# Attention block: weight products by seven instead of eight block products (Strassen), with block sums on VectorE and GpSimd

## The chip, the cores and the metric

The kernel runs on one core of one Trainium2 chip. The metric is the device time of one execution in microseconds (us); a kernel's time is the median of its runs. In the profile PE is TensorE's matmuls, PEld its weight loads, DVE is VectorE, ACT is ScalarE, POOL is GpSimd and SP is SyncE, which issues most DMAs.

## The reference

There are 16 images of 512 channels and 32 x 32 pixels, all in fp32. Each is normalised in 8 groups of channels, goes through a 1x1 convolution to q, k and v, through attention with 4 heads of 128 channels over the 1024 pixels, and through a 1x1 projection that is added to the input.

```python
xg = x.reshape(b, NUM_GROUPS, -1)
xn = ((xg - mu) * jax.lax.rsqrt(var + EPS)).reshape(b, c, h, w)
xn = xn * norm_gamma[:, None, None] + norm_beta[:, None, None]
qkv = jnp.einsum('oc,bchw->bohw', qkv_w, xn) + qkv_b[:, None, None]
...
attn = jax.nn.softmax(jnp.einsum('bhnd,bhmd->bhnm', q, k) * scale, axis=-1)
out = jnp.einsum('bhnm,bhmd->bhnd', attn, v)
...
out = jnp.einsum('oc,bchw->bohw', proj_w, out) + proj_b[:, None, None]
return x + out
```

## The kernel before

An image is held as four tiles x of 128 channels x 1024 pixels. The work is a chain of steps s, one for each image b, head h and block j of 128 keys (16 x 4 x 8 = 512 steps). A step computes the scores of a block for all 1024 queries (`scores`, L280: two matmuls of 128x512), their exponential on ScalarE (L285, tile p), the running sum of p on VectorE (L291, tile tot), and one step later the weighted sum of v (`weighted_sum`, L321: two matmuls into tile po). After the eighth block of a head `denominators` turns tot into row sums: a transpose of 32x32 blocks and a reduction on VectorE (L298, L300), a small matmul l against `fold` on PE (L302), a reciprocal r, and two DMAs that spread the reciprocals over all partitions (tile rinv). `divide` (L330) multiplies the head's output o with it.

Between the scores and the weighted sums stand the products with the weights, put there by `plan_head`, which gives each block j of a head a list of units. A unit is one PSUM bank of 512 columns with four matmuls, one for each 128 input channels: `qk_unit` (L231, tile pqk, read by ScalarE at L235), `v_unit` (L243, tile pv, read by VectorE at L248), `proj_unit` (L252, tile pp, read at L259 together with bias and residual). q and k of head h + 1 are made during head h; v and the first q and k of the next image during the last head of this one; the projection of an image during the first head of the next. All these units, the small matmul l, and the two matmuls of the normalisation's group means (pm and pv at L48 and L59, 4 columns each) share the two banks of the pool `ps_a`.

The next image's statistics come during head 2 (`stats_chunk`, `stats_group`), its normalisation at the start of head 3 (`normalise`: VectorE subtracts and scales at L71, ScalarE adds beta at L75), into tiles xn of its own, so that x stays for the residual. At the end, six projection units of the last image run with three of four matmuls before the last `divide`.

The order in which engines work is that of the program as the tile scheduler has arranged it; each engine runs its instructions in order and waits on semaphores.

```python
for s in range(steps + 1):
    if s < steps:
        ...
        scores(s)
        for u in plan[j]:
            u()
        if j == 1 and s > NB:
            divide(*where(s - NB)[:2])
    if s > 0:
        if s % NB == 0:
            denominators(*where(s - 1)[:2])
        weighted_sum(s - 1)
```

The last branch of the program (`general_path`) runs only when a flag, worked out from the row sums, asks for it.

## Time and profile before

| | |
|---|---|
| median of 3 runs | 3590.45 us (3590.2 to 3592.93) |
| the profiled execution | 3592.27 us, of which the trace spans 3590.2 us |
| PE busy | 3555.8 us, 99% of the span |
| VectorE, ScalarE, GpSimd busy | 1150.2, 824.6, 16.6 us |
| granted TensorE clock | 0.999 of full speed |
| DMA | 106.80 MB |

The span is what the trace covers; the execution's own time is 2.1 us longer. A busy share is an average over the whole span and says nothing of where an engine waits. An fp32 matmul leaves two records in the trace, one for each pass over its columns, each with a weight load of its own.

### The profile page before, as it was taken

How to read it: one execution, taken by the hardware profiler on the slowest of the kernel's cores; microseconds unless marked ns; L12 is line 12 of the kernel's file. 1: busy time of each engine (PE TensorE's matmuls, PEld its weight loads, DVE VectorE, ACT ScalarE, POOL GpSimd, SP SyncE). 2: the span in 40 equal slices, each digit the busy share in tenths (PEclk: the TensorE clock that was granted, in tenths of full speed). 3: DMA queues.
4: the chain of work that ended last, by engine and by line, in shares of the span. 5: the costliest groups of instructions: out<-in, count | busy, mean ns of one | idle time of the engine just before them, and what ended most of it. 6: DMA issues, size and time to landing. Idle time of an engine off the chain costs nothing.

```text
span 3590.2 us, 20812 instructions
## 1 busy us (share of the span) xinstructions
PE 3555.8 (99%) x8386; PEld 1567.8 (44%) x8386; DVE 1150.2 (32%) x1471; ACT 824.6 (23%) x893; POOL 16.6 (0%) x22
## 2 busy tenths in 40 slices
PE   8999999999999999999999999999999999999999
PEld 3444444444444444444444444444444444444443
DVE  2333323333232332423324233332333323233223
ACT  1221212212132121312213122131221312213121
POOL 0000000000000000000000000000000000000000
PEclk9999999999999999999999999999999999999999
DMA  2001001010000100001010010100101001010001
GB/s 73 36 12 53 12 27 38 12 53 12 30 35 12 53 12 30 36 15 50 12 38 29 16 47 12 53 18 12 53 6 59 12 15 50 6 59 12 18 24 36
DMA packets 43062, 106.80 MB, mean 30 GB/s; under 512 B 8016, under 2 KB 8016, under 8 KB 42960
## 3 DMA queue, kind: packets, MB, share of 16 engines
...
q8 instruction: 67, 1.10, 0.1%
q14 instruction: 35, 0.29, 0.0%
HBM read 71.58 MB, written 33.82 MB: 29 GB/s over the span
## 4 chain that ended last, share of the span: by engine, by line
PE 95%; DVE 2%; ACT 1%; DMA 0%; POOL 0%; issue 0%; SPq 0%; POOLq 0%
PE pqk L231 25%; PE po L321 23%; PE s L280 23%; PE pv L243 12%; PE pp L252 12%; ACT xn L75 1%; PE pp_last L252 1%; DVE tt L298 1%; DVE tot L291 1%; DVE part L300 1%; POOL rstd L63 0%; ACT p L285 0%; PE l L302 0%; DVE xn L71 0%; DMA wq<-in_qkv_wT 0%
## 5 line engine op out<-in xcount | busy, mean ns | idle before, releaser
L321 PE MATMUL po<-p,v 128*128 128x512 f32 x2048 | 972.0, 596 | 0.0
L291 DVE TENSOR_TENSOR tot<-tot,p 128x1024 f32<-128x1024 f32 x384 | 470.6, 1225 | 1565.1 <-ACT p L285 1564.9
L280 PE MATMUL s<-qk,qk 128*128 128x512 f32 x2048 | 966.4, 593 | 0.0
L285 ACT ACTIVATE p<-s 128x1024 f32<-128x1024 f32 x512 | 523.2, 1022 | 1760.5 <-PE s L280 1659.3
L280 PEld LDWEIGHTS s<-qk,qk 128*128 128x128 f32 x2048 | 387.8, 190 | 482.8 <-issue 482.2
L321 PEld LDWEIGHTS po<-p,v 128*128 128x128 f32 x2048 | 382.9, 190 | 455.0 <-issue 437.2
L231 PE MATMUL pqk<-xn,wq 128*128 128x512 f32 x1024 | 460.2, 595 | 3.8 <-DMA wproj<-in_proj_wT 3.8
L231 PE MATMUL pqk<-xn,wk 128*128 128x512 f32 x1024 | 457.7, 592 | 0.0
L243 PE MATMUL pv<-wv,xn 128*128 128x512 f32 x1024 | 449.4, 592 | 0.0
L252 PE MATMUL pp<-o,wproj 128*128 128x512 f32 x976 | 430.6, 594 | 1.5 <-DVE y L259 1.5
L235 ACT ACTIVATE qk<-pqk,qkb_sb 128x512 f32<-128x512 f32 x256 | 175.9, 687 | 838.1 <-PE pqk L231 838.1
L231 PEld LDWEIGHTS pqk<-xn,wq 128*128 128x128 f32 x1024 | 195.4, 191 | 249.7 <-issue 245.3
L231 PEld LDWEIGHTS pqk<-xn,wk 128*128 128x128 f32 x1024 | 194.6, 190 | 244.9 <-issue 244.9
L243 PEld LDWEIGHTS pv<-wv,xn 128*128 128x128 f32 x1024 | 194.6, 190 | 244.9 <-issue 244.9
L252 PEld LDWEIGHTS pp<-o,wproj 128*128 128x128 f32 x976 | 186.0, 191 | 236.3 <-issue 233.9
L259 DVE SCALAR_TENSOR_TENSOR y<-pp,projb_sb,x 128x512 f32<-128x512 f32 x122 | 91.6, 751 | 236.7 <-PE pp L252 236.7
L248 DVE TENSOR_TENSOR v<-pv,vb_sb 128x512 f32<-128x512 f32 x128 | 88.3, 690 | 231.8 <-PE pv L243 231.8
L289 DVE TENSOR_TENSOR tot<-p,p 128x1024 f32<-128x1024 f32 x64 | 78.4, 1225 | 178.6 <-ACT p L285 178.6
L39 DVE BATCH_NORM_STATS2 st<-x 128x6 f32<-128x512 f32 x128 | 80.8, 663 | 5.2 <-DMA x<-in_x 5.1
L330 DVE TENSOR_TENSOR o<-o,rinv 128x1024 f32<-128x1024 f32 x64 | 78.1, 1220 | 9.9 <-DMA rinv<-row 9.8
L327 ACT COPY o<-po 128x1024 f32<-128x1024 f32 x64 | 64.6, 1009 | 69.1 <-PE po L321 69.1
L298 DVE STREAM_TRANSPOSE tt<-tot 128x1024 f32<-128x1024 f32 x64 | 79.7, 1245 | 2.2
...
## 6 DMA issues: line engine op xcount, KB each, us to landing
...
out_y<-y SPq DMA_DIRECT2D x128, 256.0 KB, 2.0
...
```

The source lines that it names most:

```text
L39: nc.vector.bn_stats(st[:, h, :], x[:, ts(h, HALF)])
L231: nc.tensor.matmul(acc, wqkv[which][c][:, ts(h, P)], xns[b, c][:, ts(half, HALF)], start=(c == 0), stop=(c == NCC - 1),)
L235: nc.scalar.activation(store[b, h][:, ts(half, HALF)], acc, AF.Identity, bias=qkb_sb[:, o : o + 1])
L243: nc.tensor.matmul(acc[:, :C], xns[b, c][:, ts(j, P)], wqkv[2][c], start=(c == 0), stop=(c == NCC - 1),)
L248: nc.vector.tensor_add(vs[b, j], acc[:, :C], vb_sb)
L252: nc.tensor.matmul(acc, wproj[c][:, ts(o, P)], os_[b, c][:, ts(half, HALF)], start=(c == 0), stop=(c == NCC - 1),)
L259: nc.vector.scalar_tensor_tensor(y, acc, projb_sb[:, o : o + 1], xs[b, o][:, ts(half, HALF)], ALU.add, ALU.add)
L280: nc.tensor.matmul(sc[:, ts(half, HALF)], ks[b, h][:, ts(j, P)], qs[b, h][:, ts(half, HALF)], start=True, stop=True,)
L285: e = nc.scalar.activation(ps[s], sc, AF.Exp, scale=SCALE)
L291: nc.vector.tensor_add(tot[b, h], tot[b, h], ps[s])
L298: nc.vector.transpose(tt.rearrange("p c m -> p (c m)"), t)
L321: nc.tensor.matmul(po[b, h][:, ts(half, HALF)], vs[b, j][:, ts(h, P)], p[:, ts(half, HALF)], start=(j == 0), stop=(j == NB - 1),)
```

## The change

Each product with the weights is seen as a product of 2 x 2 blocks and done with seven block products in place of eight. Of the weights the blocks are a11 to a22, of the data b11 to b22 (two tiles of channels, half of the pixels); s1 to s4 and t1 to t4 are sums of them, made on VectorE for the data (`sums_of_b`, 8 adds of 128x512 for an image's x and 8 for the head outputs o), and once at the start on VectorE and GpSimd for the weights. `quad` is a group of seven products p1 to p7, each of two 128x512 matmuls (for v four of 128x256); they use the two banks of `ps_a`, and what a bank holds is read and added to others by VectorE (u2, u3 and the four results) or, for p1 and one result, ScalarE. p2, p4 and p3 add onto a bank whose first content has been read.

t1 overwrites a half of x or o; x itself is normalised in place, so `proj_units` loads x again from HBM for the residual, and GpSimd adds three of its four results. The pool of x has four tiles in place of eight, and load_x(b + 1) stands in head 2. The bias of v is multiplied with the projection at the start (16 matmuls of one column, L547) and added to that of the projection. The row sums' small matmul becomes three adds of 32x32 and a transpose on VectorE. `divide` moves to block 2. The projection at the end is done whole, after the last divide.

```diff
+FACTORS = {
+    1: ("a11", "b11"), 2: ("a12", "b21"), 3: ("s4", "b22"), 4: ("a22", "t4"),
+    5: ("s1", "t1"), 6: ("s2", "t2"), 7: ("s3", "t3"),
+}
+KC = 2
...
+def sums_of_b(eng, b):
+    for k in range(KC):
+        eng.tensor_sub(b["t3"][k], b["b22"][k], b["b12"][k])
+        eng.tensor_sub(b["t1"][k], b["b12"][k], b["b11"][k])
+        eng.tensor_sub(b["t2"][k], b["b22"][k], b["t1"][k])
+        eng.tensor_sub(b["t4"][k], b["b21"][k], b["t2"][k])
...
-    xpool = ctx.enter_context(tc.tile_pool(name="x", bufs=2 * NCC))
-    xnpool = ctx.enter_context(tc.tile_pool(name="xn", bufs=NCC))
...
+    xpool = ctx.enter_context(tc.tile_pool(name="x", bufs=NCC))
+    tpool = ctx.enter_context(tc.tile_pool(name="t", bufs=1))
...
-    ppool = ctx.enter_context(tc.tile_pool(name="p", bufs=4))
+    ppool = ctx.enter_context(tc.tile_pool(name="p", bufs=3))
...
-    def normalise(b, c):
-        xns[b, c] = xnpool.tile([P, N], F32, tag="xn", name=f"xn_{b}_{c}")
-        norm.apply(xns[b, c], xs[b, c], *scaled[b], c, b > 0)
+    def normalise(b, c, half=None):
+        t = xs[b, c] if half is None else xs[b, c][:, ts(half, HALF)]
+        norm.apply(t, t, *scaled[b], c, True)
...
+    def quad(name, mm, results, shape=None):
+        banks = {}
+        def bank(i):
+            banks[i] = ps_a.tile([P, HALF], F32, tag="acc", name=f"{name}_{i}")
+            return banks[i]
+        def p1():
+            mm(bank(1), 1, True)
+            u["p1"] = upool.tile([P, HALF], F32, tag="p1", name=f"{name}_p1")
+            nc.scalar.copy(u["p1"], banks[1])
+        def p6():
+            mm(bank(6), 6, True)
+            u[2] = upool.tile([P, HALF], F32, tag="u2", bufs=2, name=f"{name}_u2")
+            nc.vector.tensor_add(u[2], banks[6], u["p1"])
+        def p2():
+            mm(banks[1], 2, False)
+            results["c11"](banks[1])
+        def p7():
+            mm(bank(7), 7, True)
+            u[3] = upool.tile([P, HALF], F32, tag="u3", name=f"{name}_u3")
+            nc.vector.tensor_add(u[3], banks[7], u[2])
+        def p5():
+            mm(bank(5), 5, True)
+            results["c22"](banks[5], u[3])
+        def p4():
+            mm(banks[7], 4, False)
+            results["c21"](banks[7], u[2])
+        def p3():
+            mm(banks[5], 3, False)
+            results["c12"](banks[5], u[2])
+        u = {}
+        return [p1, p6, p2, p7, p5, p4, p3]
...
+    def v_units(b, jj):
+        def mm(acc, i, first):
+            wn, xn = FACTORS[i]
+            for g in range(2):
+                for k in range(KC):
+                    nc.tensor.matmul(
+                        acc[:, ts(g, HC)], xb[b][xn][k][:, ts(2 * jj + g, P)], wv[wn][k],
+                        start=(first and g == 0 and k == 0), stop=(k == KC - 1),
+                        skip_group_check=True,
...
+        def plus(which, half):
+            def f(acc, u):
+                t = upool.tile([P, HALF], F32, tag="yu", bufs=2, name=f"yu_{b}_{o}_{which}_{half}")
+                nc.vector.scalar_tensor_tensor(t, acc, bias(which), u, ALU.add, ALU.add)
+                nc.gpsimd.tensor_add(res[which, half], res[which, half], t)
+                store(which, half)
+            return f
...
-        l = ps_a.tile([P, HALF], F32, tag="acc", name=f"l_{b}_{h}")
-        nc.tensor.matmul(l[:BLK, :BLK], part, fold, start=True, stop=True)
-        r = lpool.tile([BLK, BLK], F32, tag="r", name=f"r_{b}_{h}")
-        nc.vector.reciprocal(r, l[:BLK, :BLK])
-        worst = lpool.tile([BLK, BLK], F32, tag="worst", name=f"worst_{b}_{h}")
-        i = b * HEADS + h
-        nc.vector.scalar_tensor_tensor(
-            worst, l[:BLK, :BLK], 1.0, r, ALU.mult, ALU.max, accum_out=spans[:, i : i + 1]
-        )
+        l = lpool.tile([BLK, 4, BLK], F32, tag="l", name=f"l_{b}_{h}")
+        nc.vector.tensor_add(l[:, 0, :], part[ts(0, BLK), :], part[ts(1, BLK), :])
+        nc.vector.tensor_add(l[:, 1, :], part[ts(2, BLK), :], part[ts(3, BLK), :])
+        nc.vector.tensor_add(l[:, 2, :], l[:, 0, :], l[:, 1, :])
+        nc.vector.transpose(l[:, 3, :], l[:, 2, :])
+        r = lpool.tile([BLK, BLK], F32, tag="r", bufs=2, name=f"r_{b}_{h}")
+        nc.vector.reciprocal(r, l[:, 3, :])
...
         if h == 0:
+            spread(plan, qk_units(b, 1), 0, NB)
             if b > 0:
-                spread(plan, proj_units(b - 1), 3, 7)
+                plan[3].append(lambda: o_sums(b - 1))
+                spread(plan, proj_units(b - 1, 0), 4, NB)
+        elif h == 1:
+            if b > 0:
+                spread(plan, proj_units(b - 1, 1), 0, 4)
+            spread(plan, qk_units(b, 2), 0, NB)
+        elif h == 2:
+            spread(plan, qk_units(b, 3), 0, 4)
             if b + 1 < B:
-                plan[7].append(lambda: load_x(b + 1))
-        if h + 1 < HEADS:
-            spread(plan, qk_units(b, h + 1), 0, NB)
-        if b + 1 < B:
-            if h == HEADS - 2:
-                spread(plan, [lambda c=c: stats_chunk(b + 1, c) for c in range(NCC)], 2, 6)
-                plan[6].append(lambda: stats_group(b + 1))
-            if h == HEADS - 1:
-                spread(plan, [lambda c=c: normalise(b + 1, c) for c in range(NCC)], 0, 2)
-                spread(
-                    plan,
-                    qk_units(b + 1, 0) + [lambda j=j: v_unit(b + 1, j) for j in range(NB)],
-                    2, NB,
-                )
+                plan[4].append(lambda: load_x(b + 1))
+                spread(plan, [lambda c=c: stats_chunk(b + 1, c) for c in range(NCC)], 5, 8)
+                plan[7].append(lambda: stats_group(b + 1))
+        elif b + 1 < B:
+            spread(plan, [lambda c=c: normalise(b + 1, c) for c in range(NCC)], 0, 1)
+            plan[0].append(lambda: x_sums(b + 1))
+            spread(
+                plan, qk_units(b + 1, 0) + v_units(b + 1, 0) + v_units(b + 1, 1), 1, NB
+            )
         return plan
...
+    sums_of_a(nc.vector, wqk, ts(0, P))
+    sums_of_a(nc.gpsimd, wv, slice(0, HC))
+    sums_of_a(nc.gpsimd, wqk, slice(P, C))
...
-    for acc, (o, half) in zip(accs, early):
-        proj_products(acc, B - 1, o, half, range(NCC - 1))
-    divide(B - 1, HEADS - 1)
-    for acc, (o, half) in zip(accs, early):
-        proj_products(acc, B - 1, o, half, [NCC - 1])
-        proj_store(acc, B - 1, o, half)
...
+    divide(B - 1, HEADS - 1)
+    o_sums(B - 1)
+    for u in proj_units(B - 1, 0) + proj_units(B - 1, 1):
+        u()
```

The first place is PE at the start of a last head, of image 5, where image 6 is brought in. Before (s and po are scores and weighted sums, l_2 the row sums of head 2, pqk_0_0_0 the first product of the new image's q):

```order
L280 MATMUL s_3690<-qk_5_3_3550,qk_5_3_3623 128x512 x2
L321 MATMUL po_2_3583<-p_3685,v_7_3253 128x512 x2
L280 MATMUL s_3719<-qk_5_3_3550,qk_5_3_3623 128x512
L302 MATMUL l_2_3705<-fold,part_2_3703 32x32
L280 MATMUL s_3719<-qk_5_3_3550,qk_5_3_3623 128x512
L321 MATMUL po_3_3733<-p_3693,v_0_3180 128x512 x2
L280 MATMUL s_3736<-qk_5_3_3550,qk_5_3_3623 128x512 x2
L231 MATMUL pqk_0_0_0_3743<-xn_0_3695,wq_66 128x512
L231 MATMUL pqk_0_0_0_3743<-xn_1_3698,wq_67 128x512
L231 MATMUL pqk_0_0_0_3743<-xn_2_3726,wq_68 128x512
L231 MATMUL pqk_0_0_0_3743<-xn_3_3729,wq_69 128x512
```

After (qk_0_1 and qk_0_6 are the banks of p1 and p6 of the group; what reads x_2 and x_3 into qk_0_1 is p2, and xt are sums of x):

```order
L445 MATMUL s_4398<-qk_5_3_4283,qk_5_3_4303 128x512 x2
L489 MATMUL po_2_4290<-p_4369,v_1_3822 128x512 x2
L445 MATMUL s_4446<-qk_5_3_4283,qk_5_3_4303 128x512 x2
L319 MATMUL qk_0_1_4453<-x_0_4327,wqk_a_0_128 128x512
L319 MATMUL qk_0_1_4453<-x_1_4329,wqk_a_1_129 128x512
L445 MATMUL s_4470<-qk_5_3_4283,qk_5_3_4303 128x512 x2
L319 MATMUL qk_0_6_4458<-xt_4411,wqk_s_0_138 128x512
L319 MATMUL qk_0_1_4453<-x_2_4331,wqk_a_0_130 128x512
L319 MATMUL qk_0_6_4458<-xt_4412,wqk_s_1_139 128x512
L319 MATMUL qk_0_1_4453<-x_3_4333,wqk_a_1_131 128x512
L489 MATMUL po_3_4467<-p_4401,v_1_3822 128x512 x2
L319 MATMUL qk_0_7_4477<-xt_4413,wqk_a_0_132 128x512
```

The row sums' matmul is gone, p1 stands one step earlier, and p6, which needs the sums xt, is split by halves with p2.

The second place is VectorE there. Before (sc is the last small tile of the normalisation, L71 subtracts and scales):

```order
L65 TENSOR_TENSOR sc<-rstd,gamma_sb 128x4
L71 TENSOR_SCALAR xn_0_3695<-x_0_3427,mu,sc 128x1024
L71 TENSOR_SCALAR xn_1_3698<-x_1_3429,mu,sc 128x1024
L71 TENSOR_SCALAR xn_2_3726<-x_2_3431,mu,sc 128x1024
L71 TENSOR_SCALAR xn_3_3729<-x_3_3433,mu,sc 128x1024
L291 TENSOR_TENSOR tot_2_3580<-tot_2_3580,p_3685 128x1024
L298 STREAM_TRANSPOSE tt_2_3701<-tot_2_3580 128x1024
L300 TENSOR_REDUCE part_2_3703<-tt_2_3701 128x32
```

After, behind the transpose L462 and the first three of the same four L71:

```order
L71 TENSOR_SCALAR x_3_4333<-x_3_4333,mu,sc 128x1024
L464 TENSOR_REDUCE part_2_4427<-tt_2_4425 128x32
L467 TENSOR_TENSOR l_2_4429<-part_2_4427 32x32
L468 TENSOR_TENSOR l_2_4429<-part_2_4427 32x32
L156 TENSOR_TENSOR xt_4413<-x_2_4331,x_0_4327 128x512
L469 TENSOR_TENSOR l_2_4429<-l_2_4429 32x32
L157 TENSOR_TENSOR x_0_4327<-x_0_4327 128x512
L156 TENSOR_TENSOR xt_4414<-x_3_4333,x_1_4329 128x512
L158 TENSOR_TENSOR xt_4411<-x_2_4331,x_0_4327 128x512
L157 TENSOR_TENSOR x_1_4329<-x_1_4329 128x512
L159 TENSOR_TENSOR xt_4415<-x_2_4331,xt_4411 128x512
L158 TENSOR_TENSOR xt_4412<-x_3_4333,x_1_4329 128x512
```

Between the last L71 and the sums xt_4411 and xt_4412 that p6 reads (both L158) now stand the reduction of the row sums, their small adds and the other sums of x.

The third place is PE at the end. Before (pp_last are the projection units of the last image; those of o_3, the last head, come after what is shown):

```order
L280 MATMUL s_9809<-qk_15_3_9632,qk_15_3_9696 128x512 x2
L321 MATMUL po_3_9766<-p_9804,v_6_9336 128x512 x2
L321 MATMUL po_3_9766<-p_9812,v_7_9343 128x512 x2
L252 MATMUL pp_last_9835<-o_0_9547,wproj_78 128x512
L252 MATMUL pp_last_9835<-o_1_9655,wproj_79 128x512
L302 MATMUL l_3_9821<-fold,part_3_9819 32x32
L252 MATMUL pp_last_9835<-o_2_9756,wproj_80 128x512
L252 MATMUL pp_last_9835<-o_0_9547,wproj_78 128x512
L252 MATMUL pp_last_9835<-o_1_9655,wproj_79 128x512
L252 MATMUL pp_last_9835<-o_2_9756,wproj_80 128x512
```

After (pp_0 is the first group of the projection, ot are sums of o; o_3 and ot_11658 need the last divide):

```order
L489 MATMUL po_3_11576<-p_11615,v_1_11012 128x512 x2
L489 MATMUL po_3_11576<-p_11623,v_1_11012 128x512 x2
L386 MATMUL pp_0_1_11679<-o_0_11314,wp_a_0_174 128x512
L386 MATMUL pp_0_1_11679<-o_1_11462,wp_a_1_175 128x512
L386 MATMUL pp_0_6_11684<-ot_11657,wp_s_0_184 128x512
L386 MATMUL pp_0_1_11679<-o_2_11567,wp_a_0_176 128x512
L579 MATMUL most<-ones,total 1x1
L386 MATMUL pp_0_1_11679<-o_3_11647,wp_a_1_177 128x512
L386 MATMUL pp_0_6_11684<-ot_11658,wp_s_1_185 128x512
L386 MATMUL pp_0_7_11693<-ot_11659,wp_a_0_178 128x512
L386 MATMUL pp_0_7_11693<-ot_11660,wp_a_1_179 128x512
L386 MATMUL pp_0_5_11698<-o_0_11314,wp_s_0_182 128x512
```

Eighteen matmuls stood between the last weighted sum and the first that needs the last head; now four do, and the flag's small matmul.

## Rows read from the trace of the kernel before

**Rows 1.** The page: busy share and instructions of each engine, and the chain by engine.
```profile
PE 3555.8 (99%) x8386; PEld 1567.8 (44%) x8386; DVE 1150.2 (32%) x1471; ACT 824.6 (23%) x893; POOL 16.6 (0%) x22
...
PE 95%; DVE 2%; ACT 1%; DMA 0%; POOL 0%; issue 0%; SPq 0%; POOLq 0%
```

**Rows 2.** Windows: span, then busy us (instructions) by engine, granted clock, DMA share, GB/s.
```profile
61.85:3552.77 3490.92, 3480.72 (x8219) 1534.93 (x8218) 1122.77 (x1413) 819.54 (x887) 15.10 (x15) 1.00 0.08 28
839.00:1061.59 222.59, 221.90 (x526) 97.86 (x525) 71.58 (x91) 51.70 (x56) 1.01 (x1) 1.00 0.08 29
3552.77:3590.20 37.43, 30.30 (x69) 12.58 (x67) 9.44 (x17) 1.01 (x1) 0.00 (x0) 0.95 0.20 72
3573.00:3576.30 3.30, 1.29 (x5) 0.36 (x4) 2.27 (x6) 0.00 (x0) 0.00 (x0) 0.99 0.44 164
3576.30:3579.70 3.40, 3.37 (x4) 1.51 (x5) 0.63 (x1) 0.00 (x0) 0.00 (x0) 0.51 0.64 236
```

**Rows 3.** Groups by form: record count, busy us, mean ns, idle before.
```profile
L321 PE MATMUL po<-p,v 128*128 128x512 f32 x2048 | 972.0, 596 | 0.0
...
L243 PE MATMUL pv<-wv,xn 128*128 128x512 f32 x1024 | 449.4, 592 | 0.0
```

**Rows 4.** Timeline, PE, its weight loads, and sc on VectorE: start us, us, engine, line, operation.
```profile
304.98 0.19 PEld L321 LDWEIGHTS po<-p,v 128*128 128x128 f32 x1 [0.24 <-issue]
...
305.41 0.19 PEld L321 LDWEIGHTS po<-p,v 128*128 128x128 f32 x1 [0.24 <-issue]
...
401.86 0.28 PE L48 MATMUL pm<-mean,avg 128*128 128x4 f32 x2
...
401.97 0.30 PEld L321 LDWEIGHTS po<-p,v 128*128 128x128 f32 x2
...
402.00 1.10 PE L321 MATMUL po<-p,v 128*128 128x512 f32 x2
...
403.23 1.10 PE L321 MATMUL po<-p,v 128*128 128x512 f32 x2
...
404.76 0.16 DVE L65 TENSOR_TENSOR sc<-rstd,gamma_sb 128x4 f32<-128x4 f32 x1 [1.19 <-POOL rstd L63]
```

**Rows 5.** Groups by form: durations on VectorE, ScalarE and GpSimd.
```profile
L291 DVE TENSOR_TENSOR tot<-tot,p 128x1024 f32<-128x1024 f32 x384 | 470.6, 1225 | 1565.1 <-ACT p L285 1564.9
...
L235 ACT ACTIVATE qk<-pqk,qkb_sb 128x512 f32<-128x512 f32 x256 | 175.9, 687 | 838.1 <-PE pqk L231 838.1
...
L248 DVE TENSOR_TENSOR v<-pv,vb_sb 128x512 f32<-128x512 f32 x128 | 88.3, 690 | 231.8 <-PE pv L243 231.8
...
L300 DVE TENSOR_REDUCE part<-tt 128x32 f32<-128x1024 f32 x64 | 78.1, 1220 | 2.2
...
L75 ACT ACTIVATE xn<-xn,beta_sb 128x1024 f32<-128x1024 f32 x60 | 65.5, 1139 | 45.8 <-DVE xn L71 45.8
...
L71 DVE TENSOR_SCALAR xn<-x,mu,sc 128x1024 f32<-128x1024 f32 x64 | 47.8, 809 | 0.6
...
L63 POOL TENSOR_TENSOR rstd<-ve,neghalf 128x4 f32<-128x4 f32 x16 | 16.1, 1007 | 3281.1 <-DVE ve L61 3281.1
```

**Rows 6.** Timeline: the pass after a projection unit's last starts, and VectorE reads it.
```profile
301.54 0.19 PEld L252 LDWEIGHTS pp<-o,wproj 128*128 128x128 f32 x1 [0.24 <-issue]
...
301.74 0.75 DVE L259 SCALAR_TENSOR_TENSOR y<-pp,projb_sb,x 128x512 f32<-128x512 f32 x1 [1.09 <-PE pp L252]
```

**Rows 7.** Tile x: time from a DMA's issue to its landing.
```profile
DMA to landing us min/median/max: 3.4/5.2/7.6
```

**Rows 8.** Timeline of the start: ScalarE's first instruction after its DMA issues.
```profile
15.84 1.28 ACT L235 ACT_TABLE_LOAD   x1 [15.84 <-DMA wproj<-in_proj_wT]
```

**Rows 9.** Timeline of the end: the last denominators' DMA, the divide, the last y.
```profile
3555.24 0.32 SPq L311 DMA_DIRECT2D row<-r  x1
...
3560.22 1.23 DVE L330 TENSOR_TENSOR o<-o,rinv 128x1024 f32<-128x1024 f32 x1 [4.54 <-DMA rinv<-row]
...
3585.14 0.75 DVE L259 SCALAR_TENSOR_TENSOR y<-pp,projb_sb,x 128x512 f32<-128x512 f32 x1 [2.68 <-PE pp L252]
```

More of the change, by code (lines that the diff above doesn't have):

```diff
@@ L173, in load_x @@
             eng = (nc.sync, nc.scalar)[c % 2] if b == 0 else nc.sync
[L174 to L182 removed]
+            eng.dma_start(xs[b, c], x[b, ts(c, P), :])
     load_x(0)
@@ new lines, in qk_units, with dst, bias @@
+    def qk_units(b, h):
+        def mm(acc, i, first):
+            wn, xn = FACTORS[i]
+            for k in range(KC):
+                nc.tensor.matmul(
+                    acc, wqk[wn][k][:, ts(h, P)], xb[b][xn][k],
+                    start=(first and k == 0), stop=(k == KC - 1), skip_group_check=True,
+                )
+        def dst(which, half):
+            store = (qs, ks)[which]
+            if (b, h) not in store:
+                store[b, h] = qkpool.tile(
+                    [P, N], F32, tag=f"qk{which}", name=f"qk{which}_{b}_{h}"
+                )
+            return store[b, h][:, ts(half, HALF)]
+        def bias(which):
+            return qkb_sb[:, which * HEADS + h : which * HEADS + h + 1]
+        def plus(which, half):
+            return lambda acc, u: nc.vector.scalar_tensor_tensor(
+                dst(which, half), acc, bias(which), u, ALU.add, ALU.add
+            )
+        return quad(f"qk_{b}_{h}", mm, {
+            "c11": lambda acc: nc.scalar.activation(dst(0, 0), acc, AF.Identity, bias=bias(0)),
+            "c12": plus(0, 1), "c21": plus(1, 0), "c22": plus(1, 1),
+        })
@@ new lines, in v_units, with mm, dst, view @@
+    def v_units(b, jj):
+        def mm(acc, i, first):
+            wn, xn = FACTORS[i]
+            for g in range(2):
+                for k in range(KC):
+                    nc.tensor.matmul(
+                        acc[:, ts(g, HC)], xb[b][xn][k][:, ts(2 * jj + g, P)], wv[wn][k],
+                        start=(first and g == 0 and k == 0), stop=(k == KC - 1),
+                        skip_group_check=True,
+                    )
+        def dst(pair, half):
+            if (b, pair) not in vs:
+                vs[b, pair] = vpool.tile([P, 2, NB, P], F32, tag="v", name=f"v_{b}_{pair}")
+            j = half * (NB // 2) + 2 * jj
+            return vs[b, pair][:, :, j : j + 2, :].rearrange("p h j d -> p j h d")
+        def view(t):
+            return t.rearrange("p (j h d) -> p j h d", j=2, h=2)
+        def plus(pair, half):
+            return lambda acc, u: nc.vector.tensor_add(dst(pair, half), view(acc), view(u))
+        return quad(f"v_{b}_{jj}", mm, {
+            "c11": lambda acc: nc.scalar.copy(dst(0, 0), view(acc)),
+            "c12": plus(0, 1), "c21": plus(1, 0), "c22": plus(1, 1),
+        })
```

270 lines of the change are left out of this document (143 added, 127 removed).

## Prediction

> **What bounds the kernel now.** I read the page's shares and its chain first. TensorE (PE) is busy 99% of the span and holds 95% of the chain; VectorE (DVE) has 32%, ScalarE (ACT) 23%, GpSimd (POOL) nothing [rows 1]. Next the windows: an image in the middle takes 222.59 us, of which PE is busy 221.90 [rows 2]. In the groups every 128x512 fp32 matmul counts as two (2048 records for 1024 calls), one per pass [rows 3]. In the timeline passes follow each other every 0.429 us, each with a weight load of 0.19 us inside [rows 4]. So a matmul costs 0.8576 us, the 256 of an image 219.55, and only 3.04 us of an image is anything else. From the first score (61.85) to the last weighted sum (3552.77) there are 4016 matmuls, 3444.1 us of 3490.92; 46.8 us are left. The pm/pv pair costs 0.14 us for pm and 0.37 where pv splits po (403.23 less 402.00 less two passes) [rows 4]: 7.7 us for 15 images. The other 39.1 belong to the 63 small matmuls l. PE is the limit everywhere, so what PE does not issue is gained, unless a wait takes its place.
>
> **Matmuls removed.** A group of eight block products becomes seven: 56 for 64 matmuls in q/k, 28 for 32 in v, 28 for 32 in the projection, so 240 for 256 an image. Between first score and last weighted sum 1968 weight matmuls become 1722, and 3770 x 0.8576 = 3233.2 us remain. The l matmuls go to DVE as adds of 32x32, so their 39.1 us go; between 0 and 39.1, and I take all, because nothing on PE waits for those sums any more except by the divide. The 7.7 us of pm/pv stay.
>
> **The v products** move 256 columns a pass, 840 matmuls in twice as many pieces; no row shows that form. Below: half a 512-column pass plus the 2 ns by which 0.429 exceeds twice 512 columns at the granted 2.4 GHz, 3 us in all. Above: the weight load isn't covered and each of 1680 passes pays up to 0.19 us, 319 us. The two loads after pm start 0.11 us apart (two in 0.30, 0.19 each) [rows 4], well below half a pass (0.215), so I take 2 us. The Trainium skill speaks against it: "TensorE: Matmul & The Clock Gate", Part 3, What overlaps and what doesn't, says that a weight load overlaps running matmuls only when the row group differs, and here all rows are used. By that rule halving the columns would not halve a pass, the serial rival below, some 3467 to 3535; the trace disagrees as far as it goes, since loads start inside running passes [rows 4].
>
> **The block sums and returns.** Eight sums for x and eight for the head outputs per image (0.69 us each, like the 128x512 add; the 1024 one is 1.23), and seven returns from PSUM per group (0.69 to 0.75) instead of eight reads by DVE or ACT [rows 5]. Of 56 returns 14 go to ACT. The other 42 come to DVE in place of 16 reads: per image 71.6 [rows 2] + 16 x 0.69 + 26 x 0.7 = 101 us of some 209. DVE has room; what matters is when. ACT has 14 in place of 16 and stays as it is.
>
> A return starts 0.20 us after its last pass [rows 6], takes 0.69 to 0.75, so a bank is back after 1.0 us. Two banks serve a group, and the order puts at least one other product (1.715 us) or attention work between a product and the next use of its bank. Cover is thus 0.7 us; if a sum of p (1.23) stands in front the bank is 0.5 late. I walked the new order with these durations through a whole image: through the v products, o sums and projection I find waits of 0.1 us only, because most products have 3.4 us of attention work beside them. The closest place is the projection's first group in head 0: p2 ends, DVE's c11 has its bank back 0.95 later, and p6, which takes it, stands behind two more matmuls (1.7); p7 then wants p6's bank 0.86 after p6 and waits 0.1.
>
> **The one real wait: the start of a last head.** The sums of the new image are made there. From pm = 0: PE runs po, pv, po, s, po, s and wants p1 at 7.4. In the trace sc starts 2.90 after pm and takes 0.16, like each small add [rows 4]; the 1.01 of POOL's pow [rows 5] ahead of it now hides a tot add of 1.23. So DVE has sc at 3.15, the transpose (1.23, as the reduction) at 4.4, four subtract-and-scale from 4.4 to 7.45 (0.81 each, a little overlapped), ACT's beta passes from 5.25 to 9.8 (1.14 each). x_0 and x_1 are ready at 7.5: p1 waits 0.1, ends 9.25; s to 10.97. DVE: reduce to 8.7, l adds 9.0, t3 9.7, l add 9.9, t1 10.55, t3 11.25, t2 11.95, t1 12.6, t4 13.3, t2 14.0. p6's first half waits for 11.95 (1.0 us), runs to 12.8, a half of p2 to 13.7, p6's second half waits for 14.0 (0.3). Sum 1.4 us, and 0.6 for the small waits: 2 us for each of 15 images, 30 us. Bounds: 0 (the chain hidden) and 7 an image (every sum waiting its ACT pass), 105.
>
> With x normalised in place the next image can be loaded only after q/k of head 3. Its last two chunks are issued 6.9 us after p5 of that group, land within 5.2 more, median [rows 7], and the statistics end at 14.6, when PE wants pm at 20.6. The 6 us between hide it; a load of 7.6, the longest, still fits, and each microsecond past that would cost 15. The reload for the residual goes to a core whose DMA engines are 8% busy [rows 2] and is issued a group ahead: nothing.
>
> **Start.** ACT is free of DMA issues at 15.84, then a table load of 1.28 [rows 8]. Eight half-width beta passes of 0.69 end at 22.7, sums to 26.1, then 19 products, 32.6: first score at 58.7 if clock and DMA are ideal. The 16 matmuls for the bias stand ahead of it and wait for the last projection weights; DMAs are now 128 KB. I take 64, 2 later than 61.85; bounds 59 and 72.
>
> **End.** Before, 18 early matmuls covered the wait for the last denominators; the tail is 37.43 us [rows 2]. Now, from the last weighted sum: reciprocal at 2.65, 5.0 us to landed rinv (3555.24 to 3560.22) [rows 9], divide to 8.9, sums to 11.65. PE has four matmuls and then idles 5 us; the rest run at the half clock, granted 0.51 for 3.4 us after 3.3 us in which PE was busy only 1.29 [rows 2]. Two matmuls at half clock last to 12.7, eleven products of 1.715 to 31.6, then DVE 0.95, POOL's last add, then 4.3 to the end as after the last y (3585.14 + 0.75) [rows 9]. POOL's add of 128x512 isn't in the trace: between DVE's 0.69 and four times that; I take 1.3, nearer to the POOL row of 1.01 [rows 5]. The Trainium skill ("GPSIMD Engine Reference", 3.1) has it twice as slow as DVE, which would give 1.4. Tail 38.3, 0.9 longer.
>
> **The sum.** Middle 3233.2 + 7.7 + 2 + 30 = 3272.9, 218.0 less than 3490.92. Start +2, end +0.9: 215 us less. The profiled execution took 3592.3 (span 3590.2 and 2.1 around it), so it becomes 3377; the median shown lies 1.8 lower, 3590.45, and becomes 3375.
>
> **Rivals.**
> Everything covered: no waits and an ideal start, 3375 - 30 - 5 = 3340. For it: DVE and ACT have room. Against: the chain above is 1.4 us too long by rows. 0.06.
> The clock: the waits at a last head drop it to half, as at the end; 1.7 us for a 3.4 us stretch [rows 2], once or twice an image, 26 to 51 us: 3401 to 3426. Against: in the middle it stays at 1.00 though PE waits up to 0.4 at each pv. 0.08.
> Late returns: one in four of 840 products finds a tot add in front and waits 0.5 us, 107 us: 3480, from 3430 to 3520. For: DVE has 1.23 us blocks that no one can interrupt. Against: attention work between most products. 0.15.
> Weight loads serial with the passes: then a pass of 0.429 holds 0.11 to 0.19 of load, and halving the columns saves only the rest; 0.055 to 0.095 us for each of 1680 passes, 92 to 160 us: 3467 to 3535. For: a load is in every pass. Against: the two loads 0.11 apart, and 512 columns alone fill 0.427 of 0.429 at two cycles of 2.4 GHz each. 0.05.
> Slower: the two banks decide the pace. If every product met a tot add and waited 0.51 us, 840 x 0.51 = 428: 3375 - 30 + 428 = 3773. It decides from 0.29 us a product, where 840 of them eat the gain of 215 and the 30. For: every product now returns through two banks and needs its predecessor's sum. Against: 0.7 us of cover without attention work, over 4 with it. 0.05.
> Forecast: 0.61, with its own range 3350 to 3400.
>
> **Numbers.** 0.2% (7 us) is about what a measurement of this kernel can tell from no change. All cases but the slower one and about 0.01 that falls on no change are faster: 0.94, 0.01, 0.05. The range takes the forecast, the clock, the better case and the near part of late returns: 3338 to 3450.
>
> **What would show it.** PE's pass spacing still 0.429, v passes at 0.215; no l; PE's wait for DVE's t2 at the start of a last head near 1.4 us, 15 times; granted clock 1.00 between; first score near 64; a PE gap of 5 us at the end. The prediction is wrong if PE waits for DVE or ACT more than 7 us an image, if v passes take 0.27 or more, or if the first score comes after 72.

## The result and the profile after

The changed kernel takes 3401.98 us (median of 4 runs, 3401.72 to 3402.8) against 3591.55 (3590.2 to 3592.93) of the kernel before in the same session: a ratio of 0.9473, 95% interval 0.9456 to 0.9489. The forecast was 3375, its own range 3350 to 3400, the whole range 3338 to 3450: the result lies 2 us above the one and inside the other. The gain is 190 us where 215 were worked out.

The page of the changed kernel, busy shares and chain, against [rows 1]:

```profile
PE 3342.2 (98%) x8674; PEld 1635.7 (48%) x8674; DVE 1641.3 (48%) x2408; ACT 790.8 (23%) x869; POOL 172.4 (5%) x140
...
PE 63%; issue 29%; DVE 5%; POOL 2%; DMA 1%; ACT 0%; SPq 0%; POOLq 0%; DVEq 0%
```

PE still bounds it; the 29% "issue" is time in which PE waited for nothing that the profile shows. The windows of the changed kernel cut it at the first score and behind the last weighted sum (stretch, length, busy time of PE, PEld, DVE, ACT, POOL with instructions, granted clock, DMA share, GB/s); before, the three stretches were 61.85, 3490.92 and 37.43 [rows 2]:

```profile
0.00:76.44 76.44, 48.49 (x177) 35.77 (x178) 38.12 (x66) 9.91 (x15) 22.54 (x29) 1.00 0.29 97
76.44:3360.47 3284.03, 3266.10 (x8442) 1588.82 (x8441) 1587.18 (x2314) 778.66 (x851) 142.30 (x105) 1.00 0.11 39
3360.47:3400.30 39.83, 27.63 (x59) 11.08 (x57) 15.99 (x29) 2.19 (x3) 7.58 (x6) 0.86 0.27 94
```

So the middle gained 206.9 (forecast 218.0), the start lost 14.6 (forecast 2) and the end 2.4 (forecast 0.9).

**The middle.** PE's timeline of the changed kernel (start us, us, engine, line, operation, output<-inputs, instructions, wait ahead of it and for whom), first at the start of a last head, then at the v products:

```profile
1037.46 1.88 PE L445 MATMUL s<-qk,qk 128*128 128x512 f32 x4
1040.54 1.12 PE L319 MATMUL qk<-xt,wqk_s 128*128 128x512 f32 x2 [1.20 <-DVE xt L158]
...
1056.18 1.89 PE L352 MATMUL v<-wv_a,x 128*128 128x256 f32 x8
1057.91 1.89 PE L352 MATMUL v<-wv_s,xt 128*128 128x256 f32 x8
```

Eight passes of 256 columns take 1.73 us, 0.216 each, half of the 0.429 of [rows 4]: the weight load is covered there too. The only large wait is p6's, for VectorE's sums of x. VectorE at the same place:

```profile
1032.03 0.16 DVE L65 TENSOR_TENSOR sc<-rstd,gamma_sb 128x4 f32<-128x4 f32 x1 [0.91 <-POOL rstd L63]
1032.12 1.24 DVE L462 STREAM_TRANSPOSE tt<-tot 128x1024 f32<-128x1024 f32 x1
1033.28 2.94 DVE L71 TENSOR_SCALAR x<-x,mu,sc 128x1024 f32<-128x1024 f32 x4
1036.13 1.21 DVE L464 TENSOR_REDUCE part<-tt 128x32 f32<-128x1024 f32 x1
...
1039.80 0.68 DVE L158 TENSOR_TENSOR xt<-x,x 128x512 f32<-128x512 f32 x1
```

From the transpose to t2 (L158) the instructions are those that were worked out; t2 ends 12.20 us after pm (1028.28), forecast 11.95. The chain began later than worked out: sc ends 3.91 after pm in place of 3.15. GpSimd's pow ahead of it takes 1.93 beside a sum of p on VectorE, where the forecast had its 1.01 from [rows 5]:

```profile
1030.08 1.93 POOL L63 TENSOR_TENSOR rstd<-ve,neghalf 128x4 f32<-128x4 f32 x1 [58.58 <-DVE ve L61]
```

```profile
1029.91 1.21 DVE L455 TENSOR_TENSOR tot<-tot,p 128x1024 f32<-128x1024 f32 x1
```

All but 0.25 of that was made up on the way to t2.

**The start.** VectorE of the changed kernel, a GpSimd row below it:

```profile
18.34 7.51 DVE L71 TENSOR_SCALAR x<-x,mu,sc 128x512 f32<-128x512 f32 x8
25.77 2.09 DVE L147 TENSOR_TENSOR wqk_s<-wqk_a,wqk_a 128x128 f32<-128x128 f32 x2
27.79 1.08 DVE L148 TENSOR_TENSOR wqk_a<-wqk_a,wqk_a 128x128 f32<-128x128 f32 x1
...
35.80 0.15 DVE L551 TENSOR_TENSOR projb_sb<-projb_sb,pb 128x1 f32<-128x1 f32 x1 [1.55 <-PE pb L547]
35.87 2.00 DVE L156 TENSOR_TENSOR xt<-x,x 128x512 f32<-128x512 f32 x2
```

```profile
28.68 1.04 POOL L148 TENSOR_TENSOR wqk_a<-wqk_a,wqk_a 128x384 f32<-128x384 f32 x1
```

A sum of 128x128 takes VectorE 1.08 us here, as long as the 128x384 sum that GpSimd does at that moment; and the four adds of the folded bias stand ahead of the sums of x.

### The profile page after: what moved, and what is told of

It reads as the page before. It is cut to its first block, busy times and chain, and to the rows that moved or that the text cites. A ratio compares the mean times of both kernels' runs of the same rounds, so it can differ in the third digit from the quotient of the medians.

```text
span 3400.3 us, 22944 instructions
## 1 busy us (share of the span) xinstructions
PE 3342.2 (98%) x8674; PEld 1635.7 (48%) x8674; DVE 1641.3 (48%) x2408; ACT 790.8 (23%) x869; POOL 172.4 (5%) x140
## 4 chain that ended last, share of the span: by engine, by line
PE 63%; issue 29%; DVE 5%; POOL 2%; DMA 1%; ACT 0%; SPq 0%; POOLq 0%; DVEq 0%
PE po L489 15%; PE s L445 14%; PE qk L319 13%; PE pp L386 11%; PE v L352 11%; DVE x L71 1%; POOL rstd L63 1%; DVE xt L156 1%; DVE tt L462 1%; POOL y L417 1%; DVE part L464 1%; DMA wqk_a<-in_qkv_wT 0%; ACT p L450 0%; DVE yu L416 0%; DVE tot L455 0%
## 5 line engine op out<-in xcount | busy, mean ns | idle before, releaser
L319 PE MATMUL qk<-x,wqk_a 128*128 128x512 f32 x512 | 248.4, 603 | 0.7 <-ACT qk_p L283 0.7
L319 PE MATMUL qk<-x,wqk_s 128*128 128x512 f32 x512 | 243.0, 592 | 0.0
L319 PE MATMUL qk<-xt,wqk_a 128*128 128x512 f32 x512 | 240.6, 592 | 0.0
L417 POOL TENSOR_TENSOR y<-y,yu 128x512 f32<-128x512 f32 x96 | 121.0, 1267 | 2232.2 <-DVE yu L416 2232.2
L336 DVE SCALAR_TENSOR_TENSOR qk<-qk,qkb_sb,qk_u 128x512 f32<-128x512 f32 x192 | 143.4, 747 | 28.7 <-PE qk L319 28.7
L319 PE MATMUL qk<-xt,wqk_s 128*128 128x512 f32 x256 | 127.3, 610 | 17.9 <-DVE xt L158 17.9
L386 PE MATMUL pp<-o,wp_a 128*128 128x512 f32 x256 | 122.9, 602 | 5.1 <-DVE o L498 5.1
L386 PE MATMUL pp<-ot,wp_a 128*128 128x512 f32 x256 | 122.7, 602 | 0.0
L386 PE MATMUL pp<-o,wp_s 128*128 128x512 f32 x256 | 121.9, 598 | 0.0
L352 PE MATMUL v<-wv_a,xt 128*128 128x256 f32 x512 | 121.0, 379 | 0.0
```

The source lines that it names most:

```text
L319: nc.tensor.matmul(acc, wqk[wn][k][:, ts(h, P)], xb[b][xn][k], start=(first and k == 0), stop=(k == KC - 1), skip_group_check=True,)
L336: return lambda acc, u: nc.vector.scalar_tensor_tensor(dst(which, half), acc, bias(which), u, ALU.add, ALU.add)
L352: nc.tensor.matmul(acc[:, ts(g, HC)], xb[b][xn][k][:, ts(2 * jj + g, P)], wv[wn][k], start=(first and g == 0 and k == 0), stop=(k == KC - ...
L386: nc.tensor.matmul(acc, wp[wn][k][:, ts(o, P)], ob[b][on][k], start=(first and k == 0), stop=(k == KC - 1), skip_group_check=True,)
L417: nc.gpsimd.tensor_add(res[which, half], res[which, half], t)
```

## The experiments

The changed kernel and the twelve others by stage, in us. The ratio is to the kernel before, run beside each. Start, middle and end are those of the profiled execution, which can differ from the median (all_of_it's took 3380.52).

| kernel | median | ratio, 95% interval | start | middle | end |
|---|---|---|---|---|---|
| changed kernel | 3401.98 | 0.9473, 0.9456 to 0.9489 | 76.44 | 3284.03 | 39.83 |
| v_plain | 3455.7 | 0.9625, 0.9609 to 0.9641 | 77.98 | 3335.84 | 39.68 |
| l_pe | 3414.73 | 0.9509, 0.9493 to 0.9525 | 73.80 | 3298.85 | 39.75 |
| pool_late | 3392.21 | 0.9444, 0.9428 to 0.9460 | 68.47 | 3284.05 | 40.28 |
| one_bank | 3400.62 | 0.9467, 0.9451 to 0.9483 | 73.66 | 3285.55 | 40.39 |
| start_all | 3391.20 | 0.9441, 0.9425 to 0.9457 | 65.89 | 3284.04 | 40.07 |
| tot_pool | 3498.69 | 0.9738, 0.9722 to 0.9754 | 77.36 | 3379.69 | 40.65 |
| adds_dve | 3402.95 | 0.9474, 0.9458 to 0.9489 | 77.58 | 3284.28 | 39.34 |
| later | 3396.78 | 0.9457, 0.9441 to 0.9472 | 76.78 | 3278.80 | 39.72 |
| t4_last | 3401.72 | 0.9474, 0.9458 to 0.9490 | 74.39 | 3284.25 | 40.06 |
| tail | 3398.46 | 0.9462, 0.9446 to 0.9478 | 76.35 | 3284.03 | 34.72 |
| all_of_it | 3377.21 | 0.9403, 0.9390 to 0.9416 | 60.92 | 3281.83 | 35.25 |
| last | 3375.03 | 0.9397, 0.9385 to 0.9410 | 61.19 | 3277.59 | 34.72 |

The start of six kernels whose first instructions are the same (changed kernel, tail, later, t4_last, adds_dve, tot_pool) lies between 74.39 and 77.58; a difference of less than some 3 us there says nothing. It goes with the moment at which PE's passes change from 0.85 to 0.43 us (last section): 38.71 us in t4_last, the shortest, 45.43 in adds_dve, the longest. The middle of the same order repeats within 0.3 us.

**Eight products for v again (v_plain).**

```diff
+for pair in range(2):
+    for r in range(2):
+        for k in range(KC):
+            nc.tensor.matmul(
+                acc[:, ts(pair, HC)],
+                xb[b][f"b{r + 1}{half + 1}"][k][:, ts(2 * jj + g, P)],
+                wv[f"a{pair + 1}{r + 1}"][k], ...)
```

> The v products are eight block products again in passes of 256 columns, 32 in place of 28 matmuls' worth an image (t1 and s3 stand where the overwritten blocks belong, so the values differ and the work does not). Returns of v fall from 14 of 512 columns to 8 pairs of copies of 256. Theory (TensorE's passes set the pace everywhere): 16 x 4 x 0.8576 = 54.9 more, 3455. Rival (the returns through two banks take back a part of each saved product): the loss is 20 to 40 us only, 3420 to 3440.

The middle is 51.8 longer; 15 images x 4 matmuls x 0.8576 are 51.5. A product saved is worth its passes in full, and for the v products the returns through two banks take nothing of it.

**The row sums' matmul again (l_pe).**

```diff
-        l = lpool.tile([BLK, 4, BLK], F32, tag="l", name=f"l_{b}_{h}")
-        nc.vector.tensor_add(l[:, 0, :], part[ts(0, BLK), :], part[ts(1, BLK), :])
...
+        l = ps_a.tile([P, HALF], F32, tag="acc", name=f"l_{b}_{h}")
+        nc.tensor.matmul(l[:BLK, :BLK], part, fold, start=True, stop=True)
```

> The folding of the denominators is a matmul of 32x32 again, 64 of them, with its bank from the two of the products; VectorE's three small adds and the small transpose go. Theory (what was left over in the kernel before, 39.1 us, was the price of these matmuls): 3439. Rival A (they were cheap, about 0.2 us as pm and pv are): 3413. Rival B (the matmul now waits for a reduction that stands behind the new normalise passes, and holds a bank): 1 to 2 us more at each last head, 3455 to 3470.

The middle is 14.8 longer, near the cheap rival. PE's waits of l_pe (total us, times, longest us):

```profile
PE l L471 <- DVE part L468: 11.0, 16, 1.5
```

and of the changed kernel:

```profile
PE qk L319 <- DVE xt L158: 17.9, 15, 1.2
```

p6's wait is not in l_pe's list at all: PE now waits for the reduction first, and the order has p2 ahead of p6. Both waits are for one chain: VectorE's work at the start of a last head is 0.6 us (l_pe) to 1.2 us (p6) too long for PE, whichever instruction meets it. The wait of 1.5 lies at the end of the kernel; the 15 in the middle are 9.5. Without the waits the matmuls cost 14.8 + 17.9 - 9.5 = 23.2, 0.37 each.

**GpSimd away from the start (pool_late), one bank for the bias (one_bank), both with another queue (start_all).** In pool_late a column of zeros, made from the last sum of x, is added to the weights ahead of GpSimd's sums:

```diff
+    gate = gn.tile([P, 1], F32, tag="gate", name="gate")
+    nc.gpsimd.tensor_sub(gate, xb[0]["t4"][1][:, 0:1], xb[0]["t4"][1][:, 0:1])
+    for w, at in ((wv, 0), (wqk, P)):
+        for k in range(KC):
+            t = w["a22"][k][:, at : at + 1]
+            nc.gpsimd.tensor_add(t, t, gate)
```

> GpSimd's weight sums at the start wait until VectorE has made the block sums of the first image; nothing else is changed. Theory (the two engines hold each other up there): VectorE's 128x128 weight sums fall from 1.08 us to about 0.2 and its 128x512 subtract-and-scale from about 1.0 to 0.45; x is then ready when ScalarE's last beta pass ends (28.25), the block sums run from there and the first score comes at 65 instead of 76.4: span 3389. Rival (VectorE's instructions are long by themselves, or the weights' landing sets the start): the same durations, first score at 75 to 78, span 3399 to 3402.

```diff
-                acc[:, 0:1], block[:, ts(oo, P)], vb_sb[:, c : c + 1],
+                acc[:, o : o + 1], block[:, ts(oo, P)], vb_sb[:, c : c + 1],
...
+    nc.vector.tensor_add(projb_sb, projb_sb, acc[:, 0:NCC])
```

> The four columns of the folded bias are summed into one bank and added to the bias by one instruction, in place of four banks in turn and four adds. Theory (the block sums of x stand behind the four adds, of which two wait 1.29 and 1.55 us for TensorE, which waited for a bank): block sums start at 32.8 instead of 35.87, first score 73.3, span 3397. Rival (something else, such as the last weight sum or GpSimd, sets the block sums' start): first score 76 to 77, span 3400.

```diff
-    wp = w_tiles("wp", HC, nc.scalar, ...)
+    wp = w_tiles("wp", HC, nc.sync, ...)
```

> Both of the changes above, and the eight transfers of the projection weights are issued by SyncE instead of ScalarE. Theory (after VectorE is freed, ScalarE's issue list sets the start: its table load comes at 21.94): ScalarE is free at about 16, its beta passes end at 22 to 23, the block sums at 28, first score at 59 to 60, span 3383. Rival (the landing of the weights sets the start once VectorE is free): no better than without the last step, 65, span 3389.

VectorE of start_all:

```profile
15.22 3.74 DVE L71 TENSOR_SCALAR x<-x,mu,sc 128x512 f32<-128x512 f32 x8
18.87 0.49 DVE L147 TENSOR_TENSOR wqk_s<-wqk_a,wqk_a 128x128 f32<-128x128 f32 x2
...
28.68 0.16 DVE L557 TENSOR_TENSOR projb_sb<-projb_sb,pb 128x4 f32<-128x4 f32 x1 [7.99 <-PE pb L553]
28.76 1.29 DVE L156 TENSOR_TENSOR xt<-x,x 128x512 f32<-128x512 f32 x2
```

With GpSimd still, eight L71 take 3.74 instead of 7.51, two 128x128 sums 0.49 instead of 2.09. pool_late gains 8.0 us of start and misses its 65 by 3.5: its sums of x are done 9.4 us earlier than in the changed kernel, but p6 stands behind passes that take 0.85 us each until 35.95. one_bank moves the sums of x to 33.11 as its theory has it, but they then run beside GpSimd, and its 73.66 is hardly outside the scatter (its granted clock is half once more from 39.92 to 43.34). start_all gains 2.6 over pool_late and misses its 59: its beta passes end at 22.03, but VectorE stands 7.99 us at the bias add, ahead of the sums of x, for matmuls that PE finishes late among p1's.

**The sums of p on GpSimd (tot_pool).**

```diff
-            nc.vector.tensor_add(tot[b, h], tot[b, h], ps[s])
+            nc.gpsimd.tensor_add(tot[b, h], tot[b, h], ps[s])
```

> The 448 sums of p (128x1024) run on GpSimd instead of VectorE, about 2.5 us each by the 1.27 of a 128x512 add. Theory A (the 1.23 us blocks on VectorE make returns late, about 1 us an image): these waits go, 3385. Theory B (the two engines hold each other up as at the start, and pow waits behind a sum): VectorE's block sums and returns grow by up to the length of a GpSimd add, the wait at the start of a last head grows by 3 us or more, 3440 or more.

Theory B holds. GpSimd and VectorE of tot_pool at the start of a last head:

```profile
1068.66 2.78 POOL L453 TENSOR_TENSOR tot<-p,p 128x1024 f32<-128x1024 f32 x1 [8.47 <-DVE xt L158]
1071.51 2.67 POOL L455 TENSOR_TENSOR tot<-tot,p 128x1024 f32<-128x1024 f32 x1
```

```profile
1069.14 2.84 DVE L159 TENSOR_TENSOR xt<-x,xt 128x512 f32<-128x512 f32 x1
1071.91 2.82 DVE L158 TENSOR_TENSOR xt<-x,x 128x512 f32<-128x512 f32 x1
```

A sum of 0.69 becomes 2.84 beside an add of 2.78, and the next one 2.82 beside 2.67. PE's wait for t2 grows from 17.9 to 61.8 in all, the middle by 95.7. Of these 55.3 are idle time of PE and 40.4 longer busy time: behind p6's waits, up to 4.1 us here, the granted clock falls to half once in each of the 15 last heads, 58 us in all, of which some 29 are lost (an estimate: such passes take twice as long). One of these stretches:

```profile
1075.83:1079.24 3.41, 3.41 (x6) 1.30 (x5) 3.34 (x5) 0.69 (x1) 0.00 (x0) 0.50 0.00 0
```

Instructions that read PSUM are not touched. The groups of tot_pool:

```profile
L297 DVE TENSOR_TENSOR qk_u<-qk,qk_u 128x512 f32<-128x512 f32 x64 | 44.0, 688 | 141.6 <-PE qk L319 141.6
```

against 690 ns in the changed kernel. The Trainium skill has a rule for it ("SBUF — State Buffer", SBUF: two separate sides): VectorE and GpSimd share a pair of ports; a GpSimd instruction, or a VectorE instruction that has two inputs in SBUF (against a GpSimd instruction that reads SBUF) or runs in a two-port mode, holds it to its end once it has started, while the other stops. These rows agree. The prediction did not weigh it.

**The residual adds on VectorE (adds_dve).**

```diff
-                nc.gpsimd.tensor_add(res[which, half], res[which, half], t)
+                nc.vector.tensor_add(res[which, half], res[which, half], t)
```

> The 96 residual adds of the projection run on VectorE instead of GpSimd. Theory (VectorE is under half busy and the adds are off the path): 96 x 0.69 us more on VectorE, nothing on the path, the end 0.6 us shorter: 3399 to 3402. Rival (an add in front of a return makes the bank late, 0.3 us each): 3415 to 3430.

No change in the middle: the adds lie off the path on either engine.

**The wait at the last head (later, t4_last).**

```diff
-                plan, qk_units(b + 1, 0) + v_units(b + 1, 0) + v_units(b + 1, 1), 1, NB
+                plan, qk_units(b + 1, 0) + v_units(b + 1, 0) + v_units(b + 1, 1), 2, NB
```

> The q/k and v products of the next image begin one step later in the last head (spread over six steps in place of seven). Theory (the one large wait of the middle is for the block sums at the start of a last head, 1.2 and 0.4 us, 15 times): t2 is ready before p6 reaches it, both waits go, span lower by 20 to 24: 3376 to 3380. Rival (3.5 products in a step crowd the two banks): half or all of it comes back as waits for returns, 3388 to 3400. Rival 2: the wait was not on the path, 3400.

```diff
         eng.tensor_sub(b["t2"][k], b["b22"][k], b["t1"][k])
+    for k in range(KC):
         eng.tensor_sub(b["t4"][k], b["b21"][k], b["t2"][k])
```

> Both t4 sums stand behind both t2 sums. Theory: t2 of the second chunk is ready 0.6 us earlier, the second wait of p6 (0.4 us, 15 times) goes and the first (1.2) stays: span 3394. Rival (the second wait is for something else, or t4 is then late for p4): 3399 to 3402.

In t4_last VectorE's instructions stand in the same order as without the edit, because the scheduler takes a sum that is ready; it tells nothing of the sums and is a second look at the changed kernel. In later the middle gains 5.2 of the 20 to 24, as the first rival has it. Its waits:

```profile
PE qk L319 <- DVE xt L158: 3.1, 15, 0.2
PE qk L319 <- DVE qk_u L288: 2.5, 15, 0.2
```

PE's idle time in the middle falls from 17.9 to 6.0 us (3278.80 less 3272.82 busy), but its busy time grows by 6.7 (from 3266.10): more than half of what the wait gave up came back as longer busy time, with no more matmuls to do.

**The end (tail).**

```diff
+    for early, _ in groups:
+        early()
...
+    divide(B - 1, HEADS - 1)
+    last_sums(1)
```

> For the last image the products that need no last head (p1 and p5 of both groups) are issued ahead of the last divide, into banks that the scores no longer use; t1 goes to a tile of its own. Theory (the end is TensorE's gap of 5.1 us and the half clock after it): 11 instead of 4 matmuls lie before the divide, no gap over 1 us, granted clock stays at 1.00, the stretch after the last weighted sum falls from 39.83 to 31.5, span 3392. Rival (the last returns and the store set the end, or the clock falls anyway): 36 to 40, span 3397 to 3400.

Windows of the changed kernel around its last divide, and of tail:

```profile
3364.00:3369.00 5.00, 0.26 (x3) 0.08 (x2) 1.19 (x3) 0.00 (x0) 0.00 (x0) 0.93 0.28 106
3369.40:3373.40 4.00, 3.90 (x4) 1.26 (x5) 3.39 (x5) 0.00 (x0) 0.00 (x0) 0.50 0.00 0
```

```profile
3365.00:3369.00 4.00, 3.67 (x10) 1.14 (x8) 1.21 (x3) 0.00 (x0) 0.00 (x0) 1.00 0.34 131
3369.40:3373.40 4.00, 3.65 (x8) 1.49 (x9) 3.78 (x6) 0.59 (x1) 0.00 (x0) 1.00 0.16 60
```

The gap and the half clock behind it are gone, 5.1 us of the end with them; 8.3 were expected. What is left are new waits for returns (0.35 and 0.79) and three adds of GpSimd that run one after another at the very end, 3.70 together.

**Together (all_of_it, last).** all_of_it joins the three edits of the start, with the bias folded behind the sums of x, tail (three of its adds on VectorE), later and p2 ahead of p6 in a last head:

```diff
-        return [p1, p6, p2, p7, p5, p4, p3]
+        return [p1, p2, p6, p7, p5, p4, p3] if swapped else [p1, p6, p2, p7, p5, p4, p3]
```

> Everything that moved a stage, together: GpSimd's weight sums behind the block sums, the projection weights issued by SyncE, the folded bias in one bank and now behind the block sums too (matmuls and add); in a last head p2 ahead of p6, q/k and v one step later, t4 behind t2; the early products of the last image, with its last three residual adds on VectorE. Theory (p6's wait went only in part when it was moved by one step, because t2 was late again; with p2 ahead of it t2 is ready, and no return becomes late): the start 63 in place of 76.4, the middle 3262 in place of 3284, the end 33 in place of 39.8, span 3358. Rival (each wait that is taken away in the middle comes back at the next return, as half of it did): middle 3276 to 3279, span 3373 to 3376.

The start came out better than expected, the end at 35.25 for 33, and the middle, 3281.83, came out above even its rival's 3276 to 3279: the rival's wait is there, 0.32 us at each last head for ScalarE's copy of p1, and so is one event that the changed kernel's trace doesn't have. VectorE and PE of all_of_it there:

```profile
1870.00 1.23 DVE L510 TENSOR_TENSOR o<-o,rinv 128x1024 f32<-128x1024 f32 x1 [3.94 <-DMA rinv<-row]
...
1873.73 0.75 DVE L340 SCALAR_TENSOR_TENSOR qk<-qk,qkb_sb,qk_u 128x512 f32<-128x512 f32 x1
```

```profile
1874.53 3.68 PE L323 MATMUL qk<-x,wqk_s 128*128 128x512 f32 x4 [2.34 <-DVE qk L340]
```

```profile
1874.50:1878.00 3.50, 3.47 (x4) 1.49 (x5) 1.83 (x3) 0.00 (x0) 0.00 (x0) 0.51 0.00 0
```

The divide waits in VectorE's queue for the reciprocals' DMA; when that is late (a wait of 3.94 us here, of 1.46 at 1033), the return behind it is late, PE idles 2.34 us, and four passes run at half clock. From pm to pm this image takes 212.8 us, its neighbours 208.5 and 209.0.

```diff
+            plan[1].append(units[0])
+            spread(plan, units[1:], 2, NB)
...
-            if j == 2 and s > NB:
+            if j == (3 if h == HEADS - 1 else 2) and s > NB:
```

> As the kernel with everything together, with three differences: in a last head only p1 stays in the first step and the rest, p2 first, begins one step later, so that scores and a weighted sum stand between p1 and p2 and a score no longer stands ahead of ScalarE's copy of p1; the bias is folded in head 1 of the first image, four matmuls at a time, and no longer ahead of the first score; the divide of head 2 comes one step later. Theory (the order at the start of a last head is all that the middle loses beyond small pieces): no wait of TensorE over 0.2 us at a last head, the middle 3264, the start 57.4, the end 35.3, span 3357. Rival (the wait moves to the next return again): a wait of 0.3 to 0.7 us at another product of the same step, middle 3274 to 3279, span 3367 to 3372.

It came out as its rival has it: the waits at q/k are gone, and a wait of the same size stands at the first v product, behind VectorE's divide and four sums of o. The waits of last:

```profile
PE v L355 <- DVE qk L339: 5.1, 13, 0.6
```

The start missed its 57.4 by 3.8. GpSimd's sums of the projection weights, no longer held back by the column of zeros, ran from 21.39 beside VectorE's sums of x: two of these take 2.34 there, 1.29 in all_of_it, and p6 begins 1.8 later (26.36 for 24.57). Most of the other 2 is the granted clock, which is at half from 27.86 to 31.27; two products take 5.50 there in place of 3.43:

```profile
26.00:32.00 6.00, 5.64 (x9) 2.27 (x10) 3.85 (x5) 0.00 (x0) 4.61 (x10) 0.72 0.00 0
```

all_of_it and last both beat the changed kernel, by 25 and 27 us; their intervals overlap.

## Why the prediction was right, and where it was off

**PE is the limit, a matmul costs 0.8576, 246 of them go: right**, by v_plain to 0.3 us.

**v products at half a pass plus 2 ns: right.** 1680 passes at 0.0015 over 0.2144 are 2.5 us, forecast 2. By the Trainium skill's rule on weight loads ("TensorE: Matmul & The Clock Gate", Part 3, What overlaps and what doesn't) they would have cost 92 us or more; these rows disagree with it for fp32 passes.

**The 39.1 us of the row sums' matmuls: gone from PE, but not as one price.** By l_pe 23.2 were the matmuls' own. In the kernel before 10.2 were PE's wait for the reduction:

```profile
PE l L302 <- DVE part L300: 10.2, 15, 0.7
```

A wait for that chain stands at p6 now, where the forecast priced it once more by itself. The remaining 5.7 are not told apart. The sum rested on the matmuls that remain, so the split cost it nothing.

**"0.6 for the small waits": too small in the middle.** The walk through an image found waits of 0.1 us only. A load that waits for a bank's return begins late, and the pass behind it loses 0.08 to 0.26 us that no row shows as PE's idle time. PE of the changed kernel in head 0, where groups of q/k and of the projection take turns:

```profile
1134.52 1.02 PE L319 MATMUL qk<-x,wqk_s 128*128 128x512 f32 x2
1135.46 1.98 PE L386 MATMUL pp<-ot,wp_a 128*128 128x512 f32 x4
1137.28 1.88 PE L386 MATMUL pp<-o,wp_s 128*128 128x512 f32 x4
```

From start to start two passes take 0.94 and four take 1.82, in place of 0.858 and 1.715: 0.19 is lost in these two rows, with no wait shown. A group of the projection's loads shows who is waited for (behind the bar: busy, mean ns, idle time and its releasers):

```profile
L386 PEld LDWEIGHTS pp<-o,wp_a 128*128 128x128 f32 x256 | 47.4, 190 | 68.7 <-issue 41.8 <-ACT pp_p L283 10.3 <-DVE qk L336 6.5
```

Of the middle 3284.03 - 3233.2 - 17.9 = 32.9 us are neither matmuls nor idle time at p6. By the starts of the passes in the trace, 9.0 of them are pm/pv's (0.60 an image, forecast 7.7 in all), 2.5 are v's, 5.5 are late passes around p6's wait, 13.7 are lost at five places of an image where a load waits for a return (0.91 an image), and 2.2 are spread over all passes. So the small waits took 15.9, 1.06 an image in place of 0.6. The middle is 11.1 longer than worked out: 6.9 by the small waits, 2.4 by p6, 1.3 by pm/pv and 0.5 by v.

**The one real wait: right in place and cause**, 1.2 us at p6 for VectorE's t2. Its idle time is 17.9, with the late passes around it 23.4, where 15 x 1.4 = 21 were worked out. One step ahead of it was wrong: a sum of p on VectorE does not hide GpSimd's pow but makes it longer, 1.93 for 1.01. What the text did not say, and later, all_of_it and last show, is that moving p6 did not remove the wait: each time PE waited at another product of the same head, for ScalarE's copy or for a return behind VectorE's other work.

**Start 64: wrong by 12.4**, and its sign ("wrong if the first score comes after 72") came. Two steps failed. VectorE's durations were taken from rows in which GpSimd does nothing; beside GpSimd's sums they are two to four times as long (8.0 us by pool_late, 9.4 by the time at which its sums of x are done). And ScalarE's freedom at 15.84 was carried over from [rows 8], though the change gives it 16 transfers of weights to issue in place of 8: its table load came at 21.94. That, the bias ahead of the sums of x and the clock gain 7.6 more in all_of_it, which no run parts. The clock is in it because the prediction's 58.7 held only "if clock and DMA are ideal", and in the changed kernel passes take 0.85 us until 43.72: t2 is made at 40.81, and p6 begins at 43.63, behind p2's slow passes.

**End 38.3: 39.83.** The gap is 5.12 for the 5 forecast, GpSimd's add 1.267 for the 1.3 taken; the half clock lasts from 3368.30 to 3375.13, 6.83 us where 3.4 were taken. The text's own terms add up to 38.15, not 38.3.

**Rivals.** The clock stayed at 1.00 through p6's 1.2 us. (Before the change PE's longest wait in the middle was 0.7 at l, not 0.4 at pv as that rival has it.) In tot_pool it fell behind waits of up to 4.1 us, so what the clock rival described can happen in this kernel. The total, 3401.98, lies in that rival's 3401 to 3426 by chance, since its mechanism did not occur. Returns through two banks were late by 0.08 to 0.26 us at five places of an image, not by 0.5 at one product in four. The load for the image normalised in place cost nothing: PE waits for pm's input once only, at the first image. The total came near because the errors, 12.4 at the start, 11.1 in the middle and 1.5 at the end, are small beside 211 us of removed matmuls; all have one sign, and none cancels another.
